# Four graph attention layers on one core: the first head of layer 3 takes its totals and values chunk by chunk

## The chip, the core and the metric

One core of a Trainium2 chip runs the whole program. The metric is the device time of one execution in microseconds (us), lower is better. The kernel before takes 2933.27 us, the median of three runs (2932.54 to 2933.40).

## What is computed

Sixteen graphs of 1024 nodes with 256 features pass through four attention layers. Each layer normalises its input, clips it at zero, and adds its attention's output to what came in:

```python
h = jnp.maximum(_layernorm(x, axis=-1), 0.0)
x = x + _L3_gnn_ref(h, adj, L3_gnn_W, L3_gnn_a_src, L3_gnn_a_dst, ...)
```

The change is in the last layer, which has four heads of 64 features. With an adjacency of zeros and ones, what counts of it is:

```python
h = jnp.einsum('bnd,hde->bhne', nodes_embed, W)
e_src = jnp.einsum('bhne,hte->bhtn', h, a_src)
e_dst = jnp.einsum('bhne,hte->bhtn', h, a_dst)
weight = mask * (e_src[:, :, t, :, None] + e_dst[:, :, t, None, :])
weight = jax.nn.leaky_relu(weight, negative_slope=0.01)
weight = jnp.where(node_adj[:, None] == 0, NEG, weight)
attention = jax.nn.softmax(weight, axis=-1)
dst = jnp.einsum('bhij,bhje->bhie', attention, h) + bias
out = jax.nn.relu(dst) + h      # then normalised over the head's 64 features
```

## The kernel before

**The weights.** The exponential of a leaky sum of two terms, one of the row node and one of the column node, is the larger of two products. So a block of unnormalised weights for 128 column nodes j and all 1024 row nodes i is one VectorE (DVE) instruction: a row R over i, the maximum with a column value of j, times the mask (L367, in `weigh`). R has to stand on all 128 partitions; TensorE (PE) puts it there, as eight matmuls into the PSUM tile `row`, which takes 1024 columns and has one buffer for both streams. `row_taken` keeps the order: the next row is not begun before the last weights of the present one have been issued. For heads 1 to 3 of layer 3 the row comes out of `thirds_T` with a one-hot matrix (L574): the values of R, split into three bfloat16 parts, collected in `thirds` and transposed once per batch (L640). Head 0 makes its row by broadcast transposes (L374), as the other layers do.

**Totals and values.** In layer 3 a head needs, for each node i, the sum of its weights (the total) and the sum of weights times values. Both go into an accumulator of 512 columns, `total` and `acc`. `add_values` and `add_totals` issue matmuls in which the 1024 wide block of weights is the moving operand and the stationary operand has 32 columns, so that four of them work side by side on the four quarters of the array (L586, in `in_tiles`). The eight blocks of weights are taken in two chunks of four: a chunk is 16 matmuls of values and 8 of totals. The matmuls of a chunk are pinned to program order, and all but the first of them have high priority.

**After a head.** ScalarE (ACT) copies the two accumulators to `sums` (L663), with a step of `testing` after each copy: a square over a block of the adjacency (L175), which checks that it holds zeros and ones alone. PE transposes the totals (L670) and the sums (L678); DVE inverts and multiplies (L672, L681), and `center` and `rescale` normalise.

**The order of the work.** Two streams of batches, even and odd, are issued in turns: each `yield` gives the time that a step is reckoned to take, and the stream with the earlier clock goes next; the second begins 111 us after the first. So while one batch is in layer 3, the other is in layers 0 to 2: its products with the weights (L461), the projection of its next layer (transposes L338, a copy to hT on ACT L340, matmuls L345, evictions L413 and L417). Each engine gets its instructions in one order fixed when the program is built. A scheduler decides it by priorities and dependencies, so an instruction's place in the source is not always its place in that order.

For head 0, the kernel before issues the values of chunk 1, the values of chunk 2, the transposes of `thirds`, then head 1's row (`start(behind, b)`), and after it the totals of both chunks with head 1's weights beside them. The scheduler has moved the totals of chunk 1 ahead of the values of chunk 2. Heads 1 to 3 take totals and values of a chunk together.

Of the kernel before, what the change touches and what calls it, by code (L numbers as in the profile page):

```python
# [33 lines left out]
BF = mybir.dt.bfloat16  # L34
# [7 lines left out]
P = 128  # L42
# [19 lines left out]
def short_path(ctx: ExitStack, tc: tile.TileContext, ins: dict, out: bass.AP, bad: bass.AP):  # L62

    nc = tc.nc
# [3 lines left out]
    NI = N // P  # L68
# [6 lines left out]
    QUAD = P // 4  # L75
# [7 lines left out]
    psum = ctx.enter_context(tc.tile_pool(name="psum", bufs=2, space=bass.MemoryType.PSUM))  # L83
# [15 lines left out]
    ident_bf = const.tile([P, P], BF, name="ident_bf")  # L99
# [84 lines left out]
    small = ctx.enter_context(tc.tile_pool(name="small", bufs=6))  # L184
# [111 lines left out]
    def accumulator(b: int) -> bass.AP:  # L296
        return psum.tile([P, HALF], F32, name=f"acc{b % 2}")
# [56 lines left out]
    def weigh(b: int, turn, c, op, into: list):  # L354

        while row_taken:
            yield 0.25
        row_taken.append(b)  # L360
        r = psum.tile([P, N], F32, name="row", bufs=1)
        for i in range(NI):
            turn(r[:, ts(i, P)], i)
        yield 0.5
        for j in range(NI):
            w = edges.tile([P, N], F32, name=f"weights{b % 2}")
            nc.vector.scalar_tensor_tensor(w, r, c(j), masks[b][:, j // 2, :, j % 2], op0=op, op1=ALU.mult)  # L367
            into.append(w)
            if j == NI - 1:
                row_taken.pop()  # L370
            yield 0.5

    def along_row(column):
        return lambda r, i: nc.tensor.transpose(r, column(i).to_broadcast([P, P]), ident)  # L374

    def start(behind, b: int):

        for t in behind:
            if row_taken == [b]:
                return  # L380
            yield t

    def inverse(inv: bass.AP, total: bass.AP):

        nc.vector.tensor_scalar_max(inv, total, TINY)  # L385
        nc.vector.reciprocal(inv, inv)  # L386
# [14 lines left out]
    def batch(b: int):  # L401
# [108 lines left out]
        sums = small.tile([P, NI], F32, name="sums_of_x")  # L510
# [47 lines left out]
        def rescale(yh: bass.AP, blocks, head, rstd: bass.AP, engine=nc.gpsimd):  # L558
            shape = list(yh.shape)
            nc.vector.tensor_mul(yh, yh, rstd.unsqueeze(2).to_broadcast(shape))  # L560
            engine.tensor_mul(yh, yh, gamma[:, head].unsqueeze(1).to_broadcast(shape))
            engine.tensor_add(yh, yh, xb[:, blocks, head])
# [3 lines left out]
        def weigh3(h: int):  # L566
            if h == H:
                return iter(())

            def from_thirds(r: bass.AP, i: int):  # L570

                m = i * H + h
                row = rows_of[:, m : m + 1].to_broadcast([3 * QUAD, P])
                nc.tensor.matmul(r, row, thirds_T, start=True, stop=True)  # L574

            return weigh(
                b, from_thirds if h > 0 else along_row(lambda i: ex[:, i, 2 * H : 2 * H + 1]),
                lambda j: ex[:, j, H + h : H + h + 1], ALU.max, weights,
            )

        def in_tiles(parts, accT: bass.AP, first: bool, last: bool):

            for n, (values, moving) in enumerate(parts):

                with tc.high_priority() if pinned else nullcontext():
                    made = nc.tensor.matmul(  # L586
                        accT[ts(n, QUAD), :], values, moving, start=first, stop=last
                    )
                if pinned:
                    tc.keep_in_program_order(made)  # L590
                pinned.append(made)

        def halves_of(h: int, j: int):
            return [weights[h * NI + j][:, ts(g, HALF)] for g in range(NH)]

        def add_values(h: int, j: int):

            for n in (j + 1, j):
                parts = [
                    (V3[:, n, h, ts(e, QUAD)], moving)  # L600
                    for moving in halves_of(h, n)
                    for e in range(2)
                ]
                in_tiles(parts, acc, n == 3, n == NI - 4)

        def add_totals(h: int, j: int):

            parts = [
                (V3[:, j + n, h, E:].to_broadcast([P, QUAD]), halves_of(h, j + n)[g])
                for g, n in ((0, 1), (0, 0), (1, 1), (1, 0))  # L610
            ]
            in_tiles(parts, total, j == 2, j == NI - 4)

        behind = weigh3(0)
# [4 lines left out]
        thirds = small.tile([P, 3, NI, H], BF, name="thirds", bufs=1)  # L619
# [4 lines left out]
        for h in range(H):  # L624


            acc = accumulator(b)
            total = accumulator(b)
            if h == 0:
                for first in range(0, NI, 4):  # L630
                    for _ in range(4):
                        next(behind)
                    pinned = []
                    for j in (first + 2, first):
                        add_values(h, j)
                    yield 3.6
                for _ in behind:
                    pass
                turned_thirds = psum.tile([3 * QUAD, P], BF, name="misc")
                made = nc.tensor.transpose(  # L640
                    turned_thirds, thirds.rearrange("p t i h -> p (t i h)"), ident_bf
                )
                tc.keep_in_program_order(made)
                thirds_T = small.tile([3 * QUAD, P], BF, name="thirds_T", bufs=1)
                nc.scalar.copy(thirds_T, turned_thirds)
            behind = weigh3(h + 1)
            yield from start(behind, b)

            for first in range(0, NI, 4):
                pinned = []  # L650
                for j in (first + 2, first):
                    add_totals(h, j)
                    if h > 0:
                        add_values(h, j)
                for _ in range(4):
                    next(behind, None)
                yield 1.8 if h == 0 else 5.4
            for _ in behind:
                pass
            copies = []  # L660
            for accT in (acc, total) if h == 0 else (total, acc):
                copies.append(wide.tile([P, HALF], F32, name="sums"))
                nc.scalar.copy(copies[-1], accT)  # L663
                next(testing)
                next(coming, None)
            sums, totals = copies if h == 0 else copies[::-1]
            yield 0.5
            turned = psum.tile([P, NG, P], F32, name="misc")
            for i in range(NG):
                nc.tensor.transpose(turned[:, i, :], totals[:, ts(i, P)], ident)  # L670
            inv = small.tile([P, NH, NG], F32, name="inv8", bufs=3)
            nc.vector.tensor_reduce(  # L672
                inv, turned[:, :, ::QUAD].rearrange("p i (g n) -> p g i n", n=2), AX.X, ALU.add
            )
            inverse(inv, inv)
            turned = psum.tile([P, NG, NH, E], F32, name="misc")
            for i in range(NG):
                nc.tensor.transpose(  # L678
                    turned[:, i].rearrange("p g e -> p (g e)"), sums[:, ts(i, P)], ident
                )  # L680
            nc.vector.tensor_mul(  # L681
                y[:, :, h, :].rearrange("p (g i) e -> p g i e", g=NH),
                turned.rearrange("p i g e -> p g i e"),
                inv.unsqueeze(3).to_broadcast([P, NH, NG, E]),
            )
            yield 0.5
            if h > 0:
                rescale(*normed.pop())


            if b < B - 1:
                normed.append(center(h))
            elif h < H - 1:
                normed.append(center(h, engine=nc.gpsimd if h < H - 2 else nc.vector))
            else:
                normed += [center(h, slice(g * NG, g * NG + NG), nc.vector) for g in range(NH)]
            yield 1.0
# [13 lines left out]
    def stream(first: int):  # L711
        for _ in loading[first]:
            yield 2.0
        for b in range(first, B, 2):
            yield from batch(b)
# [5 lines left out]
    while streams:  # L721
        ahead = min(streams, key=lambda s: s[0])
        t = next(ahead[1], None)
# [381 lines left out]
```

## Time and profile before

| What | Number |
|---|---|
| Time, median of 3 | 2933.27 us |
| Span of the profiled execution | 2931.4 us |
| Granted TensorE clock | 0.995 |
| PE busy | 2810.0 us (96%), 16790 matmuls |
| DVE busy | 2147.9 us (73%) |
| ACT busy | 1088.2 us (37%) |
| GpSimd busy | 981.3 us (33%) |
| Start of `thirds`' transpose, batch to batch | 178.5 us |
| L586, totals and values | 691.7 us, 6144 in the trace |
| L574, rows of heads 1 to 3 | 29.7 us, 384 in the trace |

A matmul of the program with float32 operands stands twice in the trace. Busy shares are means over the whole span. In a given stage the engine that ends last can be another than the one with the largest share, so a stage is read from its own waits. PEld is PE's load of the stationary operand; it overlaps the matmuls before it, and the distance of two loads tells the pace better than a matmul's own length, whose end is modelled.

### The profile page before, as it was taken

Reading aid. Unit: us, or ns where it says so; the run is one execution under the profiler, and the core shown is the slowest. Engines: PE = TensorE matmul, PEld = TensorE weight load, DVE = VectorE, ACT = ScalarE, POOL = GpSimd, SP = SyncE. Lnnn points to the kernel's source line nnn. Section 1 sums busy time; section 2 is a strip of 40 time slices with the busy share of each in tenths; the row PEclk is TensorE's granted clock in tenths of the full one; section 3 lists DMA queues with packets and bytes.
Section 4 is the critical chain, followed back from the end, with each engine's and each line's share of the span. In section 5 each row is a group of like instructions: output and inputs, shape, how many; then the busy total and the mean of one; then the engine's idle time right before and its main releaser. Section 6 shows DMA issues by size and latency. Waiting matters only on the chain.

```text
span 2931.4 us, 44756 instructions
## 1 busy us (share of the span) xinstructions
PE 2810.0 (96%) x16790; PEld 1961.9 (67%) x16790; DVE 2147.9 (73%) x4490; ACT 1088.2 (37%) x3010; POOL 981.3 (33%) x1533
## 2 busy tenths in 40 slices
PE   7999999999999999999999999999999999999986
PEld 5775857668576685766758577685766857667552
DVE  5658688586976859778586885868768587685857
ACT  1333434343343433424334343433434334343332
POOL 2123324243242423424233242432424224242333
PEclk9999999999999999999999999999999999999998
DMA  8204022030321303122031220303203031110101
GB/s 126 39 8 65 30 30 58 8 51 29 37 51 16 56 17 51 37 29 59 1 51 37 30 58 8 51 30 37 51 12 47 29 49 39 15 30 1 22 22 31
DMA packets 127967, 106.14 MB, mean 36 GB/s; under 512 B 79872, under 2 KB 98432, under 8 KB 127744
## 3 DMA queue, kind: packets, MB, share of 16 engines
q0 software_dynamic: 47328, 66.10, 15.4%
q1 hardware_dynamic: 79568, 35.53, 5.4%
q8 instruction: 135, 2.21, 0.3%
q10 hardware_dynamic: 848, 1.57, 0.2%
q14 instruction: 88, 0.72, 0.1%
HBM read 153.49 MB, written 33.55 MB: 64 GB/s over the span
## 4 chain that ended last, share of the span: by engine, by line
PE 59%; DVE 26%; issue 8%; POOL 3%; ACT 3%; DMA 0%; POOLq 0%; ACTq 0%; SPq 0%; DVEq 0%
PE acc L461 36%; DVE weights L367 16%; PE acc L586 10%; PE acc L345 9%; PE misc L338 2%; DVE centered L302 2%; POOL rstd L293 2%; DVE V L417 1%; PE row L374 1%; POOL y L544 1%; DVE y L545 1%; DVE var L555 1%; ACT square L309 1%; DVE y L551 1%; DVE mean L549 1%
## 5 line engine op out<-in xcount | busy, mean ns | idle before, releaser
L461 PE MATMUL acc<-V,weights 128*128 128x257 f32 x6144 | 1435.6, 384 | 33.5 <-DVE weights L367 15.7
L461 PEld LDWEIGHTS acc<-V,weights 128*128 128x128 f32 x6144 | 1136.6, 190 | 281.9 <-DVE weights L367 75.3
L586 PE MATMUL acc<-weights,V 128*32 128x512 f32 x6144 | 691.7, 596 | 12.0 <-DVE weights L367 8.1
L367 DVE SCALAR_TENSOR_TENSOR weights<-row,ex,mask 128x1024 f32<-128x1024 f32 x512 | 629.0, 1272 | 97.3 <-PE row L574 65.8
L345 PE MATMUL acc<-W,hT 128*128 128x259 f32 (+1 forms) x2048 | 516.1, 389 | 38.1 <-ACT hT L340 26.9
L367 DVE SCALAR_TENSOR_TENSOR weights<-row,V,mask 128x1024 f32<-128x1024 f32 x384 | 473.7, 1273 | 0.8 <-PE row L374 0.8
L345 PEld LDWEIGHTS acc<-W,hT 128*128 128x128 f32 x2048 | 378.7, 190 | 135.1 <-ACT hT L340 44.4
L586 PEld LDWEIGHTS acc<-weights,V 128*32 128x32 f32 x6144 | 189.1, 110 | 417.7 <-issue 410.3
L393 ACT ACTIVATE below<-acc,inv 128x256 f32<-128x256 f32 x256 | 121.1, 473 | 813.1 <-DVE inv L386 569.6
L293 POOL TENSOR_TENSOR rstd<-rstd,minus_half 128x2 f32<-128x2 f32 (+1 forms) x321 | 292.8, 912 | 20.3
L309 ACT ACTIVATE square<-x_b,minus_mean 128x256 bf16<-128x256 f32 x504 | 255.7, 507 | 110.3 <-DVE minus_mean L332 105.3
L441 POOL TENSOR_TENSOR x_b<-x_b,beta 128x256 f32<-128x256 f32 x128 | 93.5, 731 | 488.6 <-ACT square L309 483.5
L292 POOL TENSOR_SCALAR rstd<-squared 128x2 f32<-128x2 f32 x252 | 80.0, 317 | 464.0 <-ACT square L309 451.0
L385 DVE TENSOR_SCALAR inv<-acc 128x1 f32<-128x1 f32 x256 | 39.1, 153 | 255.3 <-PE acc L461 254.0
L302 DVE TENSOR_SCALAR centered<-x_b,minus_mean 128x256 f32<-128x256 f32 x504 | 195.7, 416 | 5.1
L340 ACT ACTIVATE hT<-misc 128x512 f32<-128x512 f32 x256 | 150.2, 592 | 129.6 <-PE misc L338 129.3
L396 DVE SCALAR_TENSOR_TENSOR x_b<-below,x_b 128x256 f32<-128x256 f32 x256 | 131.8, 515 | 84.9 <-ACT below L393 83.0
L663 ACT COPY sums<-acc 128x512 f32<-128x512 f32 x128 | 74.9, 585 | 308.6 <-PE acc L586 301.0
L413 ACT ACTIVATE V<-acc,rstd 128x3 f32<-128x3 f32 x384 | 98.4, 261 | 231.1 <-PE acc L345 230.6
L417 DVE TENSOR_SCALAR V<-acc,rstd,V 128x256 f32<-128x256 f32 x256 | 131.4, 537 | 59.8 <-ACT V L413 58.9
L338 PE MATMUL misc<-ident,centered 128*128 128x128 f32 x1024 | 158.7, 277 | 13.7 <-DVE centered L325 11.5
L170 POOL DMA_DIRECT2D adj_i<-in_adj_dram x128 | 74.4, 582 | 290.1 <-ACT adj_i L175 248.8
(96 smaller groups left out, 2212.8 us busy)
## 6 DMA issues: line engine op xcount, KB each, us to landing
adj_i<-in_adj_dram POOLq DMA_DIRECT2D x128, 256.0 KB, 3.9
x_b<-in_x_dram SPq DMA_DIRECT2D x15, 1024.0 KB, 6.4
narrow<-in_adj_dram POOLq DMA_DIRECT2D x60, 256.0 KB, 9.3
out_dram<-y POOLq DMA_DIRECT2D x30, 512.0 KB, 7.5
x_b<-in_x_dram ACTq DMA_DIRECT2D x4, 256.0 KB, 6.1
narrow_half<-in_adj_dram POOLq DMA_DIRECT2D x4, 256.0 KB, 16.9
mask<-narrow SPq DMA_TRANSPOSE x60, 3.7
weights<-in_L_gnn_a_dram SPq DMA_DIRECT2D x3, 256.0 KB, 5.5
```

The lines of the kernel that those rows point to most:

```text
L293: nc.gpsimd.tensor_tensor(r, r, minus_half.to_broadcast([P, n]), op=ALU.pow)
L302: nc.vector.tensor_scalar(centered[:, n, :], xb[:, 2 * pair + n, :], minus_mean[:, n : n + 1], 0.0, op0=ALU.add, op1=ALU.max,)
L309: nc.scalar.activation(square, xb[:, 2 * pair + n, :], AF.Square, bias=minus_mean[:, n : n + 1], accum_out=squared[:, n : n + 1],)
L338: nc.tensor.transpose(turned[:, k, ts(n, P)], centered[:, n, ts(k, P)], ident)
L340: nc.scalar.mul(hT, turned, ROOT_D)
L345: nc.tensor.matmul(projected, hT[:, k, ts(n, P)], W[l][:, k, :], start=(k == 0), stop=(k == NK - 1),)
L367: nc.vector.scalar_tensor_tensor(w, r, c(j), masks[b][:, j // 2, :, j % 2], op0=op, op1=ALU.mult)
L393: nc.scalar.activation(below, acc[:, :D], AF.Exp, scale=inv)
L396: nc.vector.scalar_tensor_tensor(xi, below, 1.0, xi, op0=ALU.min, op1=ALU.add)
L417: nc.vector.tensor_scalar(V[:, i, :D], projected[:, :D], rstd, V[:, i, D : D + 1], op0=ALU.mult, op1=ALU.mult,)
L461: nc.tensor.matmul(accs[i], weights[j][:, ts(i, P)], V[:, j, : D + 1], start=(j == 0), stop=(j == NI - 1),)
L586: made = nc.tensor.matmul(accT[ts(n, QUAD), :], values, moving, start=first, stop=last)
```

## The change

Head 0 takes its totals and values of a chunk together, as the other heads do, in two steps reckoned at 5.4 us instead of two at 3.6 and two at 1.8. Between the chunks the leftover weights of head 0 are issued, `thirds` is transposed, and head 1's row and its first weights are issued. The copies of the accumulators come in one order for all heads: total first, then values. No arithmetic is added or taken away. It is meant to make head 0 regular, and to have the second head's row ahead of the first head's second chunk, so that DVE can go on to the next head's weights.

```diff
             acc = accumulator(b)
             total = accumulator(b)
-            if h == 0:
-                for first in range(0, NI, 4):
+            if h > 0:
+                behind = weigh3(h + 1)
+                yield from start(behind, b)
+
+            for first in range(0, NI, 4):
+                if h == 0:
                     for _ in range(4):
                         next(behind)
-                    pinned = []
-                    for j in (first + 2, first):
-                        add_values(h, j)
-                    yield 3.6
-                for _ in behind:
-                    pass
-                turned_thirds = psum.tile([3 * QUAD, P], BF, name="misc")
-                made = nc.tensor.transpose(
-                    turned_thirds, thirds.rearrange("p t i h -> p (t i h)"), ident_bf
-                )
-                tc.keep_in_program_order(made)
-                thirds_T = small.tile([3 * QUAD, P], BF, name="thirds_T", bufs=1)
-                nc.scalar.copy(thirds_T, turned_thirds)
-            behind = weigh3(h + 1)
-            yield from start(behind, b)
-
-            for first in range(0, NI, 4):
+                if h == 0 and first > 0:
+                    for _ in behind:
+                        pass
+                    turned_thirds = psum.tile([3 * QUAD, P], BF, name="misc")
+                    made = nc.tensor.transpose(
+                        turned_thirds, thirds.rearrange("p t i h -> p (t i h)"), ident_bf
+                    )
+                    tc.keep_in_program_order(made)
+                    thirds_T = small.tile([3 * QUAD, P], BF, name="thirds_T", bufs=1)
+                    nc.scalar.copy(thirds_T, turned_thirds)
+                    behind = weigh3(1)
+                    yield from start(behind, b)
+                    for _ in range(4):
+                        next(behind)
                 pinned = []
                 for j in (first + 2, first):
                     add_totals(h, j)
-                    if h > 0:
-                        add_values(h, j)
-                for _ in range(4):
-                    next(behind, None)
-                yield 1.8 if h == 0 else 5.4
+                    add_values(h, j)
+                if h > 0 or first > 0:
+                    for _ in range(4):
+                        next(behind, None)
+                yield 5.4
             for _ in behind:
                 pass
             copies = []
-            for accT in (acc, total) if h == 0 else (total, acc):
+            for accT in (total, acc):
```

More of the change, by code (lines that the diff above doesn't have):

```diff
@@ L665, in batch @@
                 next(coming, None)
-            sums, totals = copies if h == 0 else copies[::-1]
+            totals, sums = copies
             yield 0.5
```

## The prediction, made before the change was run

> **What bounds the kernel now.** I read the page's chain that ended last first, then the row of the costliest group on the VectorE (DVE), then the timeline of one batch, and last the waits. Chain and group, from the page:
>
> ```profile
> PE 59%; DVE 26%; issue 8%; POOL 3%; ACT 3%; DMA 0%; POOLq 0%; ACTq 0%; SPq 0%; DVEq 0%
> ...
> L367 DVE SCALAR_TENSOR_TENSOR weights<-row,ex,mask 128x1024 f32<-128x1024 f32 x512 | 629.0, 1272 | 97.3 <-PE row L574 65.8
> ```
>
> TensorE (PE) is busy 96% of the span, but the chain is PE for 59% and DVE for 26%: in some stretches the making of weights ends last. The group row says what stops DVE in layer 3: 65.8 us of waiting for a row of R (L574). The list of waits spreads it: 16 waits, one per batch.
>
> ```profile
> DVE weights L367 <- PE row L574: 65.8, 16, 7.9
> ```
>
> So it is one place in each batch. The transposes of `thirds` (L640) start every 178.5 us from the second batch on (1278.87, 1457.38, 1635.88), so one batch stands for all but the last. The timeline of the one at 1457, columns start and length in us:
>
> ```profile
> 1447.82 4.86 DVE L367 SCALAR_TENSOR_TENSOR weights<-row,ex,mask 128x1024 f32<-128x1024 f32 x4 [1.79 <-PE row L374]
> ...
> 1452.80 0.19 PEld L586 LDWEIGHTS acc<-weights,V 128*32 128x32 f32 x8 [0.64 <-issue]
> ...
> 1456.40 0.74 PEld L345 LDWEIGHTS acc<-W,hT 128*128 128x128 f32 x4 [0.84 <-issue]
> ...
> 1457.53 5.36 PE L586 MATMUL acc<-weights,V 128*32 128x512 f32 x48
> ...
> 1458.84 0.13 PEld L586 LDWEIGHTS acc<-weights,V 128*32 128x32 f32 x4 [0.30 <-issue]
> ...
> 1462.81 0.45 PEld L574 LDWEIGHTS <-rows_of 96*128 96x128 bf16 x8 [0.84 <-issue]
> ...
> 1463.48 9.62 DVE L367 SCALAR_TENSOR_TENSOR weights<-row,ex,mask 128x1024 f32<-128x1024 f32 x8 [3.87 <-PE row L574]
> 1463.81 1.92 PE L586 MATMUL acc<-weights,V 128*32 128x512 f32 x16
> ...
> 1464.58 0.58 ACT L340 ACTIVATE hT<-misc 128x512 f32<-128x512 f32 x1
> ...
> 1465.67 1.61 PEld L345 LDWEIGHTS acc<-W,hT 128*128 128x128 f32 x8 [0.84 <-ACT hT L340]
> ...
> 1468.49 5.36 PE L586 MATMUL acc<-weights,V 128*32 128x512 f32 x48
> ...
> 1485.27 0.73 PEld L461 LDWEIGHTS acc<-V,weights 128*128 128x128 f32 x4 [0.99 <-DVE weights L367]
> ...
> 1486.46 0.73 PEld L461 LDWEIGHTS acc<-V,weights 128*128 128x128 f32 x4 [0.46 <-DVE weights L367]
> ...
> 1487.65 0.73 PEld L461 LDWEIGHTS acc<-V,weights 128*128 128x128 f32 x4 [0.46 <-DVE weights L367]
> ```
>
> Four of head 0's weights end at 1452.68 and the first values follow at once. The L586 matmuls go in groups of four that run side by side, 0.43 us a group (0.13 load, 0.30 gap); each matmul of the source is two in the trace, so x32 is eight groups and x48 twelve. From 1457.53 run, by the program's order, head 0's totals of chunk 1 and then its values of chunk 2. The row of head 1 comes at 1462.81 and starts eight weights after a DVE wait of 3.87 us. Head 0's totals of chunk 2 (x16, 1463.81) come **after** the row, beside those weights. DVE then runs without a gap over 0.4 us up to the last weights of the other stream, for which PE waits at 1485.27, 1486.46 and 1487.65. So here the path is: first four weights, PE up to the row, DVE for 24 us, PE again. From there PE is full again.
>
> **What the Trainium skill says.** "TensorEngine Tiling (Array Packing)", Key Properties: changing the tiling mode drains the TensorE. The trace agrees: out of a run of 32-column L586 matmuls the next weight load comes after 0.84 us instead of 0.30, and into one (after L338 at 1463.22+0.42) after 0.17: about 0.71 us per run. "PSUM — Partial Sum Buffer", Engine vs sequencer instructions: ScalarE, VectorE and GpSimd queues are strict FIFO and matmuls complete in program order. The trace agrees: nothing of DVE fills the 3.87 us before the row. So whatever stands ahead of the row in PE's order delays everything DVE does after it.
>
> **The change part by part.** The instruction order of the changed program, engine by engine, has the same instructions; it differs around head 0 in all 16 batches, and in the first 15 alike.
>
> 1. Fewer runs of L586: head 0's come as 24+24 where they came as 16+24+8 (matmuls of the source); 143 runs become 127. PE work saved: 16 x 0.71 = 11.4 us in all, if PE bounds there.
> 2. The first run has twelve groups instead of eight: 4 x 0.43 = 1.72 us more before the other stream's projection (L345) and `thirds`. The second run has twelve as before (totals and values of chunk 2 in place of totals of chunk 1 and values of chunk 2).
> 3. The row. In the source it is emitted ahead of chunk 2, but those matmuls have high priority and are pinned; in the built order the row still stands **after** chunk 2. So all 48 of head 0's matmuls are ahead of the row, where 40 were. Row at 1462.81 + 1.72, DVE's wait 3.87 + 1.72 = 5.6 us. The four groups that move ahead were hidden beside DVE's weights; they now lie on the path. A bound from both sides: 1.72 (groups only) to 0 if a wait elsewhere swallows it. I take 1.72, since the start is fixed by weight 4 (1452.68) and nothing between it and the row waits: chunk 2's weights must be ready by 1459.2, and end at 1457.98 plus the projection's eviction (L417, 0.54) now put among them, 1458.5.
> 4. After the row PE loses the 16 matmuls and a run, but stalls. On ScalarE (ACT) the copy of hT (L340) now stands behind both copies of sums and two squares of adj (1.15 and 0.19 each). From head 1's copies, which have this order (chunk at 1474.80, totals copied at 1478.56, a square, sums at 1480.22, a square to 1481.94), hT ends at chunk 2's start + 7.8. PE has row, L338 and the transposes of totals done at +6.6 (5.29+0.45+0.42+0.44), waits 1.3 us, projects (1.75), transposes sums (0.44), enters L586 (0.2 to 0.3): head 1's first chunk could begin at +10.4. Its fourth weight is there at 5.29+0.66+4.86 = +10.8. So DVE sets it, the stall costs nothing, and the saving of step 1 is not on the path either.
> 5. Head 1's start moves from 1468.49 by 1.65 to 1.75 us. PE's waits at 1485 to 1488 (0.99+0.46+0.46) remain, since DVE is as late as PE. What follows depends on these, so a batch takes 1.72 longer.
> 6. Copies of totals ahead of sums, the earlier eviction on DVE, thirds copied later: nothing, each is done microseconds before its reader (row, L672 after the eight weights).
> 7. The last batch runs alone, bound by DVE. Its row gets later by about 0.2 us (one switch fewer, weights arriving singly), but DVE's order of y's work there is changed too: between 0 and 3 us; I take 1.
>
> Sum: 15 x 1.72 + 1 = 26.8. 2933.3 + 26.8 = 2960.
>
> **The rivals.** *PE bounds everywhere.* For it: 96% busy, clock 0.995. Then step 1 counts: 2933.3 - 11.4 = 2922, faster. Against: DVE's 24 us without a gap, and PE's waits at its end. *The delay is swallowed.* PE waits for ACT and DVE elsewhere in the batch (some 7 us of the 178); were one of these set by something that doesn't move, 1.72 would vanish there: 2933. Against: no queue of DMA stands in the chain, and all other work follows the same PE and DVE queues. *ACT becomes the bound.* The hT stall grows, say through a square that waits for its DMA (1.60 us in the first batch): PE has 0.4 us at head 1 and 1.9 at 1485 in hand, so it takes 2.5 us more to lengthen a batch by some 0.6: 15 x 2.3 + 1 = 35.5, 2969.
>
> **How the numbers follow.** Forecast (row delayed by four groups) 0.78; ACT the bound 0.07; swallowed, wholly 0.05 or in part (2940 to 2950) 0.03; PE the bound 0.07. Slower 0.78+0.07+0.03 = 0.88, same 0.05, faster 0.07. Range 2950 to 2971: it holds the forecast with 0 to 3 us of the last batch and 1.2 to 2.4 us per batch, and ACT's case.
>
> **What would show it.** Right: DVE's wait for the row near 5.6 us a batch (some 92 in all), L640 at a distance of 180.2 us, first L586 run x48, a wait of about 1.3 us of L345 for hT. Wrong: row ahead of chunk 2 in the trace, distance at or under 178.5, PE not waiting for weights at the end of the stretch.

## The result and the profile after

The changed kernel takes 2964.73 us, the median of five runs (2962.43 to 2965.73), against 2933.40 us of the kernel before on the same chip (2932.54 to 2934.81): 31.3 us more, a ratio of 1.0106 with a 95% interval of 1.0091 to 1.0121. The forecast was 2960 us, in a range of 2950 to 2971.

The page of the profiled execution, its chain and the group of weights:

```profile
PE 62%; DVE 23%; issue 8%; POOL 3%; ACT 3%; DMA 0%; POOLq 0%; ACTq 0%; SPq 0%; DVEq 0%
...
L367 DVE SCALAR_TENSOR_TENSOR weights<-row,ex,mask 128x1024 f32<-128x1024 f32 x512 | 627.8, 1274 | 115.7 <-PE row L574 84.2
```

DVE's wait for the rows of heads 1 to 3 grew from 65.8 to 84.2 us, and the chain has 3 points more of PE and 3 less of DVE: the row now has more of PE's work ahead of it. PE is busy only 4.4 us longer than before (2814.4 us against 2810.0), so most of the 31.3 us is not in PE's work. The timeline of the batch that answers to the one shown before, columns start and length in us:

```profile
1466.27 0.19 PEld L586 LDWEIGHTS acc<-weights,V 128*32 128x32 f32 x8 [0.64 <-issue]
1466.31 5.36 PE L586 MATMUL acc<-weights,V 128*32 128x512 f32 x48 [0.26 <-DVE inverses L385]
...
1471.59 0.74 PEld L345 LDWEIGHTS acc<-W,hT 128*128 128x128 f32 x4 [0.84 <-issue]
...
1472.72 5.36 PE L586 MATMUL acc<-weights,V 128*32 128x512 f32 x48
...
1478.01 0.45 PEld L574 LDWEIGHTS <-rows_of 96*128 96x128 bf16 x8 [0.84 <-issue]
...
1478.67 9.63 DVE L367 SCALAR_TENSOR_TENSOR weights<-row,ex,mask 128x1024 f32<-128x1024 f32 x8 [5.05 <-PE row L574]
...
1479.77 0.58 ACT L340 ACTIVATE hT<-misc 128x512 f32<-128x512 f32 x1
...
1480.41 1.61 PEld L345 LDWEIGHTS acc<-W,hT 128*128 128x128 f32 x8 [1.13 <-ACT hT L340]
...
1483.58 0.16 PEld L586 LDWEIGHTS acc<-weights,V 128*32 128x32 f32 x8 [0.95 <-DVE weights L367]
...
1500.47 0.73 PEld L461 LDWEIGHTS acc<-V,weights 128*128 128x128 f32 x4 [1.05 <-DVE weights L367]
...
1501.66 0.73 PEld L461 LDWEIGHTS acc<-V,weights 128*128 128x128 f32 x4 [0.46 <-DVE weights L367]
...
1502.85 0.73 PEld L461 LDWEIGHTS acc<-V,weights 128*128 128x128 f32 x4 [0.46 <-DVE weights L367]
```

Read it from the first load of head 0 (1466.27; 1452.80 before). Both of head 0's runs are x48, the first 5.32 us to the next load (1471.59) where it was 3.60. The row's first load is some 11.7 us after the start (10.0 before). Head 1's first chunk begins after 17.31 us instead of 15.69, and the load that opens it waited for DVE's weights. The three waits at the stretch's end are still there (1.05, 0.46, 0.46): the last of them is 36.58 us after the start instead of 34.85. Every mark from the row on is 1.6 to 1.7 us late. The transposes of `thirds` follow each other every 180.23 us instead of every 178.50.

### The profile page after: what moved, and what is told of

The parts are those of the page before. It is cut to its first block, busy times and chain, and to the rows that moved or that the text cites. A ratio compares the mean times of both kernels' runs of the same rounds, so it can differ in the third digit from the quotient of the medians.

```text
span 2963.0 us, 44769 instructions
## 1 busy us (share of the span) xinstructions
PE 2814.4 (95%) x16790; PEld 1968.0 (66%) x16790; DVE 2149.3 (73%) x4490; ACT 1089.1 (37%) x3010; POOL 981.2 (33%) x1533
## 4 chain that ended last, share of the span: by engine, by line
PE 62%; DVE 23%; issue 8%; POOL 3%; ACT 3%; DMA 0%; POOLq 0%; ACTq 0%; SPq 0%; DVEq 0%
PE acc L461 36%; DVE weights L367 14%; PE acc L586 13%; PE acc L345 9%; PE misc L338 2%; DVE centered L302 2%; POOL rstd L293 2%; PE row L374 1%; POOL y L544 1%; DVE y L545 1%; DVE var L555 1%; DVE V L417 1%; DVE y L551 1%; DVE mean L549 1%; ACT below L393 1%
## 5 line engine op out<-in xcount | busy, mean ns | idle before, releaser
L586 PE MATMUL acc<-weights,V 128*32 128x512 f32 x6144 | 690.2, 597 | 26.0 <-DVE weights L367 22.1
L367 DVE SCALAR_TENSOR_TENSOR weights<-row,ex,mask 128x1024 f32<-128x1024 f32 x512 | 627.8, 1274 | 115.7 <-PE row L574 84.2
L345 PE MATMUL acc<-W,hT 128*128 128x259 f32 (+1 forms) x2048 | 517.8, 390 | 52.0 <-ACT hT L340 40.8
L586 PEld LDWEIGHTS acc<-weights,V 128*32 128x32 f32 x6144 | 192.7, 110 | 439.8 <-issue 417.4
L345 PEld LDWEIGHTS acc<-W,hT 128*128 128x128 f32 x2048 | 379.6, 191 | 140.1 <-ACT hT L340 49.2
L393 ACT ACTIVATE below<-acc,inv 128x256 f32<-128x256 f32 x256 | 121.1, 473 | 813.7 <-DVE inv L386 569.3
L417 DVE TENSOR_SCALAR V<-acc,rstd,V 128x256 f32<-128x256 f32 x256 | 132.9, 538 | 66.5 <-ACT V L413 65.6
L338 PE MATMUL misc<-ident,centered 128*128 128x128 f32 x1024 | 158.9, 277 | 13.5 <-DVE centered L325 11.0
```

Of the source, the lines that this page charges most:

```text
L338: nc.tensor.transpose(turned[:, k, ts(n, P)], centered[:, n, ts(k, P)], ident)
L345: nc.tensor.matmul(projected, hT[:, k, ts(n, P)], W[l][:, k, :], start=(k == 0), stop=(k == NK - 1),)
L393: nc.scalar.activation(below, acc[:, :D], AF.Exp, scale=inv)
L417: nc.vector.tensor_scalar(V[:, i, :D], projected[:, :D], rstd, V[:, i, D : D + 1], op0=ALU.mult, op1=ALU.mult,)
L586: made = nc.tensor.matmul(accT[ts(n, QUAD), :], values, moving, start=first, stop=last)
```

## The experiments

The table counts from the first load of head 0's chunk 1, in the same batch of each trace, as subtracted from the timelines. *Row* is the first load of head 1's row, *head 1* the first load of its first chunk, *L374* that of the other stream's row, *last weight* the end of the last of that stream's eight weights, *distance* that of the transposes of `thirds` from batch to batch. The last column is the median of all runs of a version; each was timed beside the kernel before on its chip, which took 2933.4 to 2933.7 us there, and the ratios below are to that.

| Kernel | row | head 1 | L374 | last weight | distance | total |
|---|---|---|---|---|---|---|
| before | 10.02 | 15.69 | 20.98 | 34.80 | 178.50 | 2933.4 |
| changed | 11.73 | 17.31 | 22.60 | 36.53 | 180.23 | 2964.7 |
| totals of chunk 2 behind the row | 10.02 | 16.39 | 21.68 | 34.89 | 178.59 | 2935.1 |
| all totals in chunk 2 | 11.73 | 17.31 | 22.59 | 36.53 | 180.23 | 2963.3 |
| eight matmuls more ahead | 13.45 | 19.02 | 24.31 | 38.24 | 181.93 | 2991.6 |
| row first | 6.69 | 15.61 | 20.90 | 33.31 | 177.01 | 2907.8 |
| squares later | 11.73 | 17.31 | 22.59 | 36.52 | 180.24 | 2968.8 |
| before, row first | 6.53 | 15.92 | 21.20 | 33.30 | 177.24 | 2910.1 |
| row first, thirds first | 6.05 | 13.12 | 20.60 | 34.20 | 179.19 | 2941.0 |

**Is it the number of matmuls ahead of the row?** Three runs vary it. The first keeps the changed chunk 1 and moves the totals of chunk 2 behind the row:

```diff
+                    pinned = [made]
+                    for j in (first + 2, first):
+                        add_values(h, j)
                     behind = weigh3(1)
...
-                pinned = []
-                for j in (first + 2, first):
-                    add_totals(h, j)
-                    add_values(h, j)
+                if h > 0 or first == 0:
+                    ...                      # the four lines above
+                else:
+                    pinned = [made]
+                    for j in (first + 2, first):
+                        add_totals(h, j)
```

> Head 0's chunk 1 stays as in the changed kernel (totals and values together), but chunk 2 is split: its values ahead of head 1's row, its totals pinned behind the row. Then 40 matmuls stand ahead of the row, as before the change, though copies are in the changed order. Theory (four groups ahead of the row cost 1.72 us a batch on DVE's path): distance of the transposes of thirds back to 178.5 us, DVE's wait for the row back to about 3.3 to 3.9 us, total 2933 to 2939 (the last batch's order may still differ). Rival (what costs is that chunk 1 is longer, or ACT's new order of copies and squares): distance stays near 180.2, total near 2960 to 2965.

It took 2935.07 us, a ratio of 1.0004 (0.9995 to 1.0013).

```profile
1463.26 0.45 PEld L574 LDWEIGHTS <-rows_of 96*128 96x128 bf16 x8 [0.84 <-issue]
1463.82 1.92 PE L586 MATMUL acc<-weights,V 128*32 128x512 f32 x16
1463.93 9.62 DVE L367 SCALAR_TENSOR_TENSOR weights<-row,ex,mask 128x1024 f32<-128x1024 f32 x8 [3.34 <-PE row L574]
```

The x16 stands beside DVE's weights again, and DVE waits 3.34 us. The longer chunk 1 and the copies' new order are still there; with all else that differs from the kernel before they come to 0.09 us a batch (178.59 against 178.50).

The second puts all totals of head 0 into chunk 2, so that the cut is another and 48 matmuls stay ahead:

```diff
+                if h == 0 and first > 0:
+                    for j in (2, 0):
+                        add_totals(h, j)
                 for j in (first + 2, first):
-                    add_totals(h, j)
+                    if h > 0 or first > 0:
+                        add_totals(h, j)
                     add_values(h, j)
```

> Chunk 1 of head 0 has values alone, chunk 2 has all totals of head 0 and its values, all ahead of head 1's row: runs of 16 and 32 matmuls, 48 ahead of the row, as many runs as in the changed kernel. Theory: only the number ahead of the row counts, not how the chunks are cut, so the distance is 180.2 us and the total 2960 to 2967. Rival (the longer chunk 1 with its later eviction is the cause): distance back to 178.5, total near 2935.

2963.33 us, 1.0104 (1.0087 to 1.0121), and row, head 1 and last weight as in the changed kernel to a hundredth. With 48 ahead of the row, how the chunks are cut doesn't matter here.

The third does chunk 1's totals twice:

```diff
+                if h == 0 and first == 0:
+                    for j in (2, 0):
+                        parts = [
+                            (V3[:, j + n, h, E:].to_broadcast([P, QUAD]), halves_of(h, j + n)[g])
+                            for g, n in ((0, 1), (0, 0), (1, 1), (1, 0))
+                        ]
+                        in_tiles(parts, total, j == 2, j == 0)
```

> The changed kernel with chunk 1's totals of head 0 done twice (the first time into the accumulator that the second time starts anew): eight more matmuls, four more groups of 0.43 us, ahead of the row. Theory: another 1.72 us a batch, distance 181.95 us, total 2964.7 + 15 x 1.72 + 0 to 2 = 2990 to 2993. Rival (PE's waits behind the row or ACT set the batch, so that work ahead of the row is partly absorbed): distance under 181, total 2965 to 2980.

2991.62 us, 1.0195 (1.0178 to 1.0212). The distance grew by 1.70 us over the changed kernel, for four groups of 0.43. Work put ahead of the row is paid in full. Taken alone, this run would also fit a PE that bounds everywhere, since it adds work to PE; the first of the three tells the two apart, because it moves matmuls and adds none.

**The row where the source has it.** The first matmul of a chunk is not pinned, so the whole chunk can pass the row. One more pin holds it:

```diff
-                pinned = []
+                pinned = [made] if h == 0 and first > 0 else []
```

> The changed kernel with the first matmul of head 0's chunk 2 pinned behind head 1's row, so that the row is ahead of the chunk in PE's order too, as the source has it. Theory: DVE's wait for the row shrinks from 5.05 to about 0.5 us and its weights start some 4.7 us earlier; PE, with a short wait for the copy of thirds, reaches head 1's first chunk about 15.7 us after head 0's (17.3 in the changed kernel, 15.7 before). From there the other stream's row (L374) behind that chunk binds DVE, so the distance becomes 178.0 to 178.5 us and the total 2925 to 2937. Rival (DVE's start is not what matters): distance stays at 180.2, total 2965.

2907.76 us, 0.9910 (0.9894 to 0.9927), faster than both kernels and than the expectation. Its timeline in the same batch:

```profile
1448.79 0.43 PEld L574 LDWEIGHTS <-rows_of 96*128 96x128 bf16 x7 [0.17 <-issue]
...
1449.32 5.36 PE L586 MATMUL acc<-weights,V 128*32 128x512 f32 x48
...
1449.43 9.63 DVE L367 SCALAR_TENSOR_TENSOR weights<-row,ex,mask 128x1024 f32<-128x1024 f32 x8 [0.27 <-PE row L574]
...
1462.66 0.69 DVE L545 SCALAR_TENSOR_TENSOR y<-y,h 128x512 f32<-128x512 f32 x1 [1.39 <-POOL y L544]
1462.72 0.85 PEld L374 LDWEIGHTS row<-ident,V 128*128 128x128 f32 x8 [0.84 <-issue]
1463.39 0.69 DVE L549 TENSOR_REDUCE mean<-y 128x8 f32<-128x512 f32 x1
...
1466.72 8.42 DVE L367 SCALAR_TENSOR_TENSOR weights<-row,V,mask 128x1024 f32<-128x1024 f32 x7
1469.03 5.93 PEld L461 LDWEIGHTS acc<-V,weights 128*128 128x128 f32 x28 [0.84 <-issue]
```

DVE waits 0.27 us and is through with head 1's weights at 1459. What the expectation had not seen is what it does with the time won: while the other stream's row (L374) is still to come, it works on head 0's output (L545, L549, L550, L551), which before stood between that stream's weights. So seven of these now follow without a gap, the last one ends 1.5 us sooner after the start than before, and PE's three waits at the end shrink to one of 0.23 us. The row comes 5.0 us sooner than in the changed kernel, but a batch is only 3.2 us shorter: what stands ahead of the row no longer sets the pace alone.

**Is ACT's new order part of the loss?** In the changed kernel L345 waits for hT, which was the place of a rival. This version takes the two squares away from between head 0's copies:

```diff
                 nc.scalar.copy(copies[-1], accT)
-                next(testing)
+                if h > 0:
+                    next(testing)
...
+            if h == 0:
+                next(testing)
+                next(testing)
             yield 1.0
```

> The changed kernel without a step of the adjacency's check between head 0's two copies and behind them: its two squares come after head 0 instead. On ACT the copy of hT then stands behind the two copies alone. Theory (DVE's fourth weight sets head 1's start, PE's wait of 1.3 us for hT lies beside it): that wait nearly goes and the distance stays at 180.2 us; total 2960 to 2965 (the first batch, where a square waits for its transfer, may give back up to 1.5 us). Rival (ACT's order is part of the loss): distance 178.9 to 179.5, total 2943 to 2954.

```profile
1485.37 1.61 PEld L345 LDWEIGHTS acc<-W,hT 128*128 128x128 f32 x8 [0.49 <-ACT hT L340]
...
1489.19 0.16 PEld L586 LDWEIGHTS acc<-weights,V 128*32 128x32 f32 x8 [1.60 <-DVE weights L367]
```

The wait for hT fell from 1.13 to 0.49 us, and the wait for weights that follows it rose from 0.95 to 1.60: the same time, under another name. The distance is 180.24 us. The total, 2968.75 us (1.0118, 1.0102 to 1.0133), missed its range by 4 us, all of it in the first batch, whose distance is 188.05 us instead of 182.72. In that batch ACT stops at a square whose block of the adjacency has not arrived, and what the other stream needs of ACT (L393, L395) stands behind it:

```profile
241.16 1.15 ACT L175 ACTIVATE adj_i<-adj_i,minus_half 128x1024 bf16<-128x1024 bf16 x1 [6.96 <-DMA adj_i<-in_adj_dram]
244.42 7.85 PE L461 MATMUL acc<-V,weights 128*128 128x257 f32 x23 [3.90 <-ACT above L395]
```

PE waits 3.90 us there, and the mean granted clock from 240 to 252 us is 0.72. So moving the squares put a new wait into the first batch; in the others it changed nothing.

**The last batch.** With head 0 of the last batch in the old form, and the copies' order with it:

```diff
+            if b < B - 1:
+                ...
+            else:
+                ...                      # the block of the kernel before
...
-            for accT in (total, acc):
+            early = h == 0 and b == B - 1
+            for accT in (acc, total) if early else (total, acc):
```

> The changed kernel with the last batch's head 0 in the form of the kernel before. In the traces the stretch from the transpose of thirds in the batch before the last to the end took 227.9 us changed and 224.2 before. If that is the changed order in the last batch: the stretch is 224.2 again and the total 2959.5 to 2962. If it comes from what the other batches leave behind (a lower clock after longer waits): it stays near 227.9, total 2964 to 2966.

The stretch from the last `thirds` transpose but one to the end took 224.5 us, where the changed kernel took 227.9 and the kernel before 224.2; the total was 2960.43 us (1.0090, 1.0076 to 1.0104). So the changed order within the last batch costs 3.4 us of the 31.3. The traces show where the time goes. Head 1's first run of L586 in the last batch, in the kernel before, in the changed kernel (with the window around it; 0.67 is the granted clock), and in this version:

```profile
2870.56 5.36 PE L586 MATMUL acc<-weights,V 128*32 128x512 f32 x48 [1.37 <-DVE weights L367]
...
2899.31 8.16 PE L586 MATMUL acc<-weights,V 128*32 128x512 f32 x48 [4.17 <-DVE weights L367]
...
2899.00:2908.00 9.00, 8.69 (x60) 2.62 (x63) 7.32 (x11) 0.00 (x0) 1.27 (x1) 0.67 0.08 15
...
2895.47 7.05 PE L586 MATMUL acc<-weights,V 128*32 128x512 f32 x48 [1.37 <-DVE weights L367]
```

With head 0's chunk 2 gone from beside DVE's weights, PE waits 4.17 us there instead of 1.37, and the run takes 8.16 us instead of 5.36. That is 2.8 us, and it comes with the lower clock. That the longer wait lowered the clock is not shown: in the old form the wait is 1.37 us and the run takes 7.05 all the same. Which of the changed moves does it was not taken apart.

**What a run of L586 costs.** The row ahead in the kernel before, with its own cut into four runs:

```diff
-                for first in range(0, NI, 4):
...
+                for j in (2, 0):
+                    add_values(h, j)
...
             behind = weigh3(h + 1)
             yield from start(behind, b)
+            if h == 0:
+                pinned = [made]
+                for j in (6, 4):
+                    add_values(h, j)
+                yield 3.6
```

> The kernel before with head 1's row placed ahead of the values of head 0's chunk 2: in the built order 16+8 of head 0's matmuls, the row, then 16 and 8, in four runs where the row-first version of the changed kernel has two. DVE is no longer held by the row. Theory: PE then bounds this stretch, and the two more runs cost it 2 x 0.71 = 1.4 us a batch: distance 177.0 + 1.4 = 178.4, total about 2929. Rival (the row's place is all, runs cost nothing): distance 176 to 177.2, total 2895 to 2908.

2910.12 us, 0.9918 (0.9902 to 0.9933): the gain belongs to the row's place, not to the cut of the chunks. But 178.4 was wrong, and so was the price of 0.71 us that it rests on. The distance is 0.23 us over the row-first version's, for two more runs. Part of it may be hidden by `thirds`, whose transpose stands here ahead of chunk 1. The lengths of the runs give the price better: to the first load of the next line a run of twelve groups takes 5.32 us, of eight 3.60, of four 1.85 (11.02 to 12.87 in the kernel before), which is 0.43 a group and 0.13 to 0.16 a run; entering after L338 adds 0.15 (0.59 from the start of its four loads, which take 0.11 each). That is about 0.3 us a run, an estimate from these distances.

**Thirds still earlier.** The row-first version with the transpose of `thirds` traced before chunk 1:

```diff
-                if h == 0 and first > 0:
-                    for _ in behind:
-                        pass
+                if h == 0 and first == 0:
                     turned_thirds = psum.tile([3 * QUAD, P], BF, name="misc")
                     ...
                     nc.scalar.copy(thirds_T, turned_thirds)
+                if h == 0 and first > 0:
+                    for _ in behind:
+                        pass
                     behind = weigh3(1)
...
-                pinned = []
+                pinned = [made] if h == 0 and first > 0 else []
```

> The row-first version with the transpose of thirds ahead of head 0's chunk 1, so that PE does not wait for the copy of thirds_T (about 0.2 to 0.3 us a batch in the row-first trace). The built order also puts the other stream's projection (L345) behind head 1's first chunk. Expected: distance 176.6 to 177.0, total 2901 to 2908, at or a little under the row-first version's 2907.8; more than that only if the projection behind the chunk removes another wait.

```profile
1454.02 0.24 POOL L623 TENSOR_TENSOR thirds<-rest,thirds 128x32 bf16<-128x32 f32 x1
1454.32 0.12 PEld L639 LDWEIGHTS <-thirds 128*96 128x96 bf16 x1 [1.73 <-POOL thirds L623]
```

2941.01 us, 1.0025 (1.0015 to 1.0035): 33 us worse than the row-first version. The built order has the transpose between the other stream's products, where GpSimd is not done with `thirds`, and PE's loads stand still for 1.73 us (its matmuls for 1.32). The transposes of sums moved behind head 1's first chunk, so the work on the output fell back between the other stream's weights, and the last of them ends at 34.20 instead of 33.31. PE's three waits at the end of the stretch are back (0.71, 0.46 and 0.46 us). A wait of 0.2 us was taken away and larger ones put in.

## Why the prediction was right, and where it was off

- **The path.** First four weights, PE up to the row, DVE, PE again: shown by the three runs that vary what stands ahead of the row. The distance follows it: 178.59 with 40 matmuls, 180.23 with 48, 181.93 with 56. With 24 (row first) it is 177.01, so below 40 it no longer falls by the full price.
- **Step 2 and 3, four groups, 1.72 us.** Measured 1.73 (178.50 to 180.23). That the row stays behind the chunk in the built order was the step that decided the sign: with the row ahead the same code is 0.9% faster than before.
- **Step 3, DVE's wait.** Forecast 5.6 us, measured 5.05: the second eviction of the projection (L417, 0.55 us) now falls into the wait instead of ahead of it. It changes where DVE idles, not when the row comes.
- **Step 4, hT beside DVE's weights.** Right: L345's matmuls waited 0.90 us and its loads 1.13 (1.3 forecast), and the run without the squares gained nothing from its end.
- **Step 1, the price of a run.** Too high. The gap of 0.84 us in PE's loads was set against 0.30 within a run, but loads run ahead of their matmuls by a group within a run (a run's first entry is x8, two groups' loads at once, and each later one x4); part of the gap is the last group's own work. Of the 0.71 us about 0.3 is lost. It was not on the path, so only the rival in which PE bounds everywhere was too fast: 16 x 0.3 = 4.8 us instead of 11.4.
- **The sum.** 26.8 us forecast, 31.6 in the spans of the two profiles. Both of its terms came out too low, so no error hid another. By the starts of `thirds`' transpose: up to the batch before the last 27.9 us instead of 15 x 1.72 = 25.8. Some 1.4 of the 2.1 missing are the first batch's. There the square waits 1.62 us for its transfer and L345 waits for hT, which was named as ACT's rival; the wait came in this batch, but what cost time was the clock. L345 in the first batch, in the changed kernel, in the version with the old last batch and in that with all totals in chunk 2:

```profile
217.90 3.07 PE L345 MATMUL acc<-W,hT 128*128 128x259 f32 x8 [2.50 <-ACT hT L340]
...
217.63 2.02 PE L345 MATMUL acc<-W,hT 128*128 128x259 f32 x8 [2.67 <-ACT hT L340]
...
217.75 2.02 PE L345 MATMUL acc<-W,hT 128*128 128x259 f32 x8 [2.63 <-ACT hT L340]
```

  The wait is alike in all three, but only in the first does the work behind it take longer. The first distance is 182.72 us in the changed kernel and 181.40 in both others, one of which has the changed kernel's own code for this batch: 1.3 us. The granted clock shows in three stretches of the changed kernel (the last three columns are granted clock, DMA share and GB/s); in the two others it is 1.00 from 216 to 224 us:

```profile
200.00:216.00 16.00, 15.14 (x126) 6.62 (x124) 10.47 (x17) 3.85 (x11) 2.08 (x4) 1.00 0.21 34
216.00:224.00 8.00, 6.10 (x32) 3.53 (x36) 8.00 (x7) 2.38 (x6) 0.00 (x0) 0.79 0.01 2
224.00:240.00 16.00, 15.94 (x115) 8.08 (x108) 13.90 (x20) 1.80 (x3) 4.25 (x5) 1.00 0.00 0
```

- **Step 7, the last batch.** 1 us forecast in a bound of 0 to 3; 3.8 measured (227.9 less 224.2), 3.4 of it given back by the old form. This is the term that was mis-sized most. The forecast looked for it in DVE's order of y's work; 2.8 us of it lie in one run of PE at a lower clock, which no step reckoned with.

## What to carry to other kernels

Where several engines take turns, look for the instruction that releases the next one, and count what stands ahead of it in its own queue: here four groups of matmuls moved ahead of one broadcast row cost their full length per batch, though PE's total work was the same. Look for it in the built order, not in the source; a chunk whose first instruction isn't pinned can pass the one it was meant to follow, and one pin was worth 1.9% between two versions of the same code. An engine that is released sooner gains most if it has other work to pull into the time won; of these runs, the row-first one shows it.

## What the runs showed of the hardware

A wait of PE can be followed by a lower clock, and then it costs more than its length. In the first batch of the changed kernel PE had no matmul for 2.50 us; the granted clock was 0.79 from 216 to 224 us, and the last loads of L345 came every 0.43 us instead of every 0.22. After waits of 3.90 us (squares later, first batch) and 4.17 us (changed kernel, last batch) the mean was 0.72 over 12 us (240 to 252) and 0.67 over 9 (2899 to 2908). The length of a wait did not decide it: after 2.67 and 2.63 us in the first batch of two other versions the clock stayed at 1.00, and in the last batch of one of these a run of L586 behind a wait of 1.37 us was slowed (7.05 us instead of 5.36, clock 0.79 from 2895 to 2903 us).

A gap in the record of weight loads is not all idle time of the array: with 0.84 us between loads at the end of a run of 32-column matmuls, the run took about 0.15 us more than its groups (5.32 us for twelve of 0.43).
